# Three kinds of PSUM evictions, written as ScalarE's

## The chip, the cores and the metric

One core of a Trainium2 chip runs the whole program. Five engines share it, each with an in-order instruction queue of its own: TensorE (PE in the profile, with its weight loads as PEld), VectorE (DVE), ScalarE (ACT), GpSimd (POOL) and SyncE (SP, which here only issues DMAs). The metric is the device time of one execution in microseconds; the median over several runs counts.

## What is computed

Two sequences of 1024 positions with 256 features pass through four residual blocks, each behind a layer norm: causal attention with 16 heads of width 128 and ALiBi slopes, a gated FFN with ternary weights, a Mamba block (a state space with 512 channels and 16 states), and a gated FFN that keeps the two largest of every four hidden values.

```python
def reference(...):
    x = L0_attn_resid_pre                                   # (2, 1024, 256), fp32
    x = x + _L0_attn_ref(_layernorm(x), Wq, Wk, Wv, Wo)
    x = x + _L0_ffn_ref(_layernorm(x), w_gate_up, w_proj)
    x = x + _L1_attn_ref(_layernorm(x), in_proj, conv1d, x_proj, dt_proj, ...)
    x = x + _L1_ffn_ref(_layernorm(x), w_gate, w_up, w_down)
    return x

# attention, the block that the change touches
q, k, v = (resid_pre @ W.T).reshape(b, s, H, DH)            # for Wq, Wk, Wv
scores = clip(einsum('bqhd,bkhd->bhqk', q, k) / sqrt(DH), -1024, 1024)
attn = softmax(scores + alibi_mask)
z = einsum('bhqk,bkhd->bqhd', attn, v)
out = einsum('bqhd,ohd->bqo', z, Wo.reshape(d, H, DH))
```

## The kernel before

The 2048 positions are cut into four chunks `k` of 512 (two for each sequence; the second one of a sequence has `u = 1` and attends to twice as many keys). Attention runs over 64 heads, chunk by chunk (`attention`). The other three blocks of a chunk (`rest`: `ternary_ffn`, `state_space`, `kept_two_ffn`) are interleaved with the attention of the next chunk: the main loop gives attention one query tile of 128 positions and then lets `rest` go on until its share of a hand-written cost is spent. While chunk 0 is in attention, the ternary weights are quantized instead. The `rest` of the last chunk has no attention beside it and forms the tail.

For one query tile `j` of a head, `scores` makes the products on TensorE (L362), clips them on VectorE into `ss` (L366), adds the bias and takes the row maximum on VectorE (L372, `nm`) and the exponential on ScalarE (L377). Two tiles later `turn` transposes these weights on TensorE, block by block (L293, into a PSUM bank `pt`), and copies each bank to SBUF, `pT` (L296): one copy of up to four 128-blocks, or two copies where a row has more than four. After the fourth tile `values` multiplies `v` and `pT` (L304, bank `z`) and copies the bank to `zs` (L309). `project` multiplies `zs` with `wo` (L318) and adds to the residual on VectorE (L324). `qkv` makes `q`, `k` and `v` of the next head (L335, L342); `q` and `k` leave their banks by a ScalarE activation (L338), `v` by a copy (L347).

The banks of `pt`, `z`, `o`, `pq`, `pk` and `pv` are one ring of three (`ps_mm`), those of `s` a ring of two, and the banks of the other blocks a ring of two (`ps_r`). In a gated FFN (`glu`) the gate and the up product take one bank each of `ps_r`: the next gate product waits until ScalarE has read this one (L446, Silu into `sg`), the next up product until VectorE has multiplied (L447). In `ternary_ffn` ScalarE then also makes the high half `hh` (L479) and the squares `sq` (L483, L486), and the products take both halves `hh` and `hl`. In `state_space` each of 64 steps takes an exponential on ScalarE (`da`, L750), a scan on VectorE (`hs`, L757) and two products on GpSimd (`db` L736, `hc` L771).

ScalarE's functions live in table sets. Silu (L446, L629, L632) is in another set than the exponential (L377, L750), and where they alternate in ScalarE's queue the compiler puts a table load in front (ACT_TABLE_LOAD). No load stands in front of a plain copy in this trace.

The order within each queue is not written out by hand. The tracer of the tile framework schedules the recorded instructions on an estimate of its own, and an instruction that was written for "any" engine is given to ScalarE or to VectorE by this schedule. Beside the three lines of the change, the turned layer norm (L148), `dtls` (L643) and `bc` (L656) are copies for "any" engine too.

Of the kernel before, what the change touches and what calls it, by code (L numbers as in the profile page):

```python
# [17 lines left out]
P = 128  # L18
# [23 lines left out]
def kernel(  # L42
# [21 lines left out]
    nc = tc.nc  # L64
# [221 lines left out]
    def turn(k, h, j, s, st):  # L286

        qi = CH[k][1] * UT + j
        for kb0 in range(0, qi + 1, 4):
            n = min(4, qi + 1 - kb0)  # L290
            tp = ps_mm(f"pt_{k}_{h}_{j}_{kb0}").rearrange("p (c t) -> p c t", c=4)
            for i in range(n):
                nc.tensor.transpose(  # L293
                    tp[:, i, :], s[:, (kb0 + i) * P : (kb0 + i + 1) * P], ident
                )
            nc.any.tensor_copy(st["pts"][kb0 // 4][:, 0:n, j * P : (j + 1) * P], tp[:, 0:n, :])  # L296

    def values(k, h, st):
        u = CH[k][1]
        zp = ps_z(f"z_{k}_{h}")  # L300
        last = (u + 1) * UT - 1
        for kb in range(last + 1):
            q0 = max(0, kb - u * UT) * P
            nc.tensor.matmul(  # L304
                zp[:, q0:], lhsT=st["v_all"][:, kb, :],
                rhs=st["pts"][kb // 4][:, kb % 4, q0:], start=(kb == 0), stop=(kb == last),
            )
        st["z"] = a2.tile([P, U], F32, tag="z", name=f"zs_{k}_{h}")
        nc.any.tensor_copy(st["z"], zp)  # L309

    def project(k, h, st):

# [15 lines left out]
    def qkv(k, h, st, xT):  # L328
        u = CH[k][1]
        st["qT"] = a2.tile([P, U], F32, tag="qT", name=f"qT_{k}_{h}")  # L330
        kT = st["kT"][:, u * U : (u + 1) * U]
        for n, dst, scale in (("q", st["qT"], -1.0 / math.sqrt(DH)), ("k", kT, 1.0)):
            pp = ps_mm(f"p{n}_{k}_{h}")
            for c in range(KC):
                nc.tensor.matmul(  # L335
                    pp, lhsT=st[n][:, c, :], rhs=xT[:, c, :], start=(c == 0), stop=(c == KC - 1)
                )
            nc.scalar.activation(dst, pp, AF.Copy, scale=scale)  # L338
        vp = ps_mm(f"pv_{k}_{h}").rearrange("p (t m) -> p t m", t=UT)
        for t in range(UT):  # L340
            for c in range(KC):
                nc.tensor.matmul(  # L342
                    vp[:, t, :], lhsT=xT[:, c, t * P : (t + 1) * P], rhs=st["v"][:, c, :],
                    start=(c == 0), stop=(c == KC - 1),
                )
        v = st["v_all"][:, u * UT : (u + 1) * UT, :]
        nc.any.tensor_copy(v, vp)  # L347
        if u < NU - 1:
            kd = dr.tile([P, U], F32, tag="kd", name=f"kd_{k}_{h}", bufs=H)
            nc.sync.dma_start(out=kd, in_=kT)  # L350
            vd = dr.tile([P, UT, DH], F32, tag="vd", name=f"vd_{k}_{h}", bufs=H)
            nc.sync.dma_start(out=vd, in_=v)
            kept[CH[k][0], h] = kd, vd
# [28 lines left out]
    def attention():  # L382
# [3 lines left out]
        for k in range(1, len(CH)):  # L386
            load_x(k)
        qkv(0, 0, live[0], xns[0])
        later = []
        for i, (k, h) in enumerate(heads):  # L390
# [8 lines left out]
            for j in range(UT):  # L399
                s = scores(k, h, j, st)  # L400
                later.append((LAG, lambda a=(k, h, j, s, st): turn(*a)))
                if j == UT - 1:
                    later.append((LAG, lambda a=(k, h, st): values(*a)))
                    later.append((LAG + 1, lambda a=(k, h, st): project(*a)))
                if j == UT - 1 and h == H - 1:
                    for _, f in later:
                        f()
                    later = []
                else:
                    now = [f for n, f in later if n == 0]  # L410
                    later = [(n - 1, f) for n, f in later if n]
                    for f in now:
                        f()
                if j == 1 and i + 1 < len(heads):
                    qkv(*heads[i + 1], live[0], xns[heads[i + 1][0]])
                if j == 0 and h == H - 1 and k + 1 < len(CH):

                    with tc.issue_after(tiles[-UT].ins) if k == 0 else nullcontext():
                        normed(k + 1)
                yield k  # L420
# [627 lines left out]
```

## Time and profile before

| what | value |
| --- | --- |
| median of 3 runs (range) | 1835.89 us (1833.85 to 1839.79) |
| span of the profiled execution | 1836.9 us |
| ACT busy, DVE busy, POOL busy | 963.7 (52%), 1218.3 (66%), 832.2 us (45%) |
| L309 `zs` copies, ACT and DVE | 52 and 12 |
| L347 `v` copies, ACT and DVE | 58 and 6 |
| DVE time of the copies, L296, L309, L347 | 35.31, 8.27, 4.13 us |
| table loads before L377, before L446 | 28 and 26, 1283 ns each |
| HBM traffic | 138 GB/s over the span |

The busy share of an engine is a mean over stages with different limits, so the profile is read in stages. The stages follow from the lines: the ternary FFN of chunk 0 has its gate and up products from 243.8 to 278.6 us, that of chunk 2 from 1135.5 to 1164.9 us; the scans of the state space run from about 363.7 to 588.2 us (chunk 0), 832.6 to 1013.5 us (chunk 1) and 1252.4 to 1476.2 us (chunk 2); the tail begins at about 1613 us. A matmul's record is longer than the time after which the next one can start, so TensorE's true need is counted from start to start.

### The profile page before, as it was taken

The numbers are of one execution on the slowest core, as the hardware profiler recorded it, in microseconds if no ns is written. First come the engines' busy times: TensorE is split into PE (matmuls) and PEld (weight loads), VectorE is DVE, ScalarE is ACT, GpSimd is POOL, SyncE is SP. The second block draws the span as 40 slices with busy tenths as digits, with TensorE's granted clock in tenths as the row PEclk, the third lists the DMA queues.
The fourth block names the chain that finished last, engine by engine and source line by source line (L and its number), as shares of the span: only waits on it lengthen the run. The fifth ranks groups of instructions, "written<-read, shape, count | busy, mean of one in ns | idle before, by whom it ended". The sixth has DMA issues, their size and how long they took to land. (4 is left out here: it accounts for less than half of the span.)

```text
span 1836.9 us, 24217 instructions
## 1 busy us (share of the span) xinstructions
PE 1718.3 (94%) x7956; PEld 1144.2 (62%) x7956; DVE 1218.3 (66%) x2349; ACT 963.7 (52%) x1789; POOL 832.2 (45%) x674
## 2 busy tenths in 40 slices
PE   7999999998999999998888999999999999998899
PEld 4666666555656557755555667756656565566895
DVE  5666555777785473458886565557788655667975
ACT  3444474656563553555554545566555446446742
POOL 3324032588892000419998000418898500035870
PEclk9999999999999999999999999999999999999999
DMA  6443512466662311337787324227665430212541
GB/s 201 128 142 128 193 46 88 149 203 204 216 202 91 103 52 48 125 109 232 245 247 224 116 71 141 82 67 228 226 214 184 142 115 26 75 53 86 178 136 57
DMA packets 178301, 255.99 MB, mean 139 GB/s; under 512 B 16240, under 2 KB 90992, under 8 KB 177152
## 3 DMA queue, kind: packets, MB, share of 16 engines
q1 hardware_dynamic: 176752, 241.61, 41.4%
q0 software_dynamic: 1152, 12.58, 1.9%
q8 instruction: 63, 1.03, 0.2%
q14 instruction: 62, 0.51, 0.1%
q10 hardware_dynamic: 272, 0.26, 0.0%
HBM read 232.04 MB, written 22.35 MB: 138 GB/s over the span
## 5 line engine op out<-in xcount | busy, mean ns | idle before, releaser
L771 POOL TENSOR_TENSOR hc<-hs,cs 128x512 f32<-128x512 f32 x256 | 362.1, 1428 | 10.8 <-DVE ss L366 3.1
L362 PE MATMUL s<-kT,qT 128*128 128x512 f32 (+3 forms) x768 | 302.7, 495 | 19.9 <-DVE ss L366 18.0
L377 ACT ACTIVATE ss<-ss,nm 128x128 f32<-128x128 f32 (+7 forms) x256 | 198.8, 776 | 183.5 <-DVE nm L372 174.1
L366 DVE SCALAR_TENSOR_TENSOR ss<-s,lower 128x512 f32<-128x512 f32 (+3 forms) x384 | 204.6, 549 | 121.0 <-PE s L362 119.4
L736 POOL TENSOR_TENSOR db<-du,bs 128x512 f32<-128x512 f32 x192 | 259.2, 1356 | 44.4 <-DVE hs L757 30.6
L304 PE MATMUL z<-pT,v 128*128 128x512 f32 (+3 forms) x768 | 264.5, 492 | 10.9 <-ACT pT L296 10.2
L372 DVE CUSTOM_DVE_ANT_0 ss<-ss,alibi 128x128 f32<-128x128 f32 (+7 forms) x256 | 241.3, 945 | 3.5
L750 ACT ACTIVATE da<-dl,a_neg 128x512 f32<-128x512 f32 x256 | 177.9, 698 | 115.6 <-DVE hs L757 90.6
L304 PEld LDWEIGHTS z<-pT,v 128*128 128x128 f32 x768 | 142.8, 190 | 145.1 <-issue 92.7
L296 ACT COPY pT<-pt 128x512 f32<-128x512 f32 (+3 forms) x321 | 145.4, 474 | 162.0 <-PE pt L293 160.4
L293 PE MATMUL pt<-ident,ss 128*128 128x128 f32 x1152 | 180.3, 279 | 32.1 <-DVE x L324 18.5
L293 PEld LDWEIGHTS pt<-ident,ss 128*128 128x128 f32 x1152 | 140.0, 142 | 94.7 <-DVE x L324 33.0
L362 PEld LDWEIGHTS s<-kT,qT 128*128 128x128 f32 x768 | 127.9, 193 | 84.1 <-issue 43.4
L757 DVE TENSOR_TENSOR_SCAN hs<-da,db 128x512 f32<-128x512 f32 x128 | 153.8, 1210 | 38.6 <-ACT da L750 20.8
L757 DVE TENSOR_TENSOR_SCAN hs<-da,carry,db 128x512 f32<-128x512 f32 x128 | 159.1, 1269 | 24.4 <-POOL hc L771 14.7
L324 DVE SCALAR_TENSOR_TENSOR x<-o,rr,x 128x256 f32<-128x256 f32 x256 | 108.9, 476 | 76.7 <-PE o L318 76.5
L701 PE MATMUL y<-ident,hc 128*128 128x128 f32 x1024 | 144.8, 279 | 8.4 <-POOL hc L771 8.4
L342 PEld LDWEIGHTS pv<-wv,xT_a 128*128 128x128 f32 x1024 | 124.4, 192 | 37.1 <-issue 25.3
L342 PE MATMUL pv<-wv,xT_a 128*128 128x128 f32 x1024 | 125.8, 275 | 5.5 <-ACT zs L309 3.4
L701 PEld LDWEIGHTS y<-ident,hc 128*128 128x128 f32 x1024 | 121.0, 145 | 14.3 <-POOL hc L771 11.9
L318 PE MATMUL o<-wo,zs 128*128 128x256 f32 x512 | 125.4, 386 | 4.1 <-ACT kT L338 3.0
L335 PE MATMUL pq<-xT_a,wq 128*128 128x512 f32 x256 | 122.7, 601 | 0.7 <-ACT xT_a L148 0.7
(204 smaller groups left out, 2468.7 us busy)
## 6 DMA issues: line engine op xcount, KB each, us to landing
cs<-bcd SPq DMA_DIRECT2D x256, 256.0 KB, 3.8
bs<-bcd SPq DMA_DIRECT2D x192, 256.0 KB, 4.3
alibi<-alibi_d SPq DMA_DIRECT2D x32, 512.0 KB, 4.2
wq<-in_wqT_dram SPq DMA_DIRECT2D x64, 128.0 KB, 3.5
wk<-in_wkT_dram SPq DMA_DIRECT2D x64, 128.0 KB, 3.1
wv<-in_wvT_dram SPq DMA_DIRECT2D x64, 128.0 KB, 2.8
wo<-in_woT_dram SPq DMA_DIRECT2D x64, 128.0 KB, 2.8
alibi<-alibi_d SPq DMA_DIRECT2D x32, 256.0 KB, 3.6
```

The lines of the kernel that those rows point to most:

```text
L293: nc.tensor.transpose(tp[:, i, :], s[:, (kb0 + i) * P : (kb0 + i + 1) * P], ident)
L304: nc.tensor.matmul(zp[:, q0:], lhsT=st["v_all"][:, kb, :], rhs=st["pts"][kb // 4][:, kb % 4, q0:], start=(kb == 0), stop=(kb == last),)
L342: nc.tensor.matmul(vp[:, t, :], lhsT=xT[:, c, t * P : (t + 1) * P], rhs=st["v"][:, c, :], start=(c == 0), stop=(c == KC - 1),)
L362: nc.tensor.matmul(sp[:, :n], lhsT=st["qT"][:, j * P : (j + 1) * P], rhs=st["kT"][:, k0 : k0 + n], start=True, stop=True,)
L366: nc.vector.scalar_tensor_tensor(s[:, k0 : k0 + n], sp[:, :n], CLIP, lower[:, S - W + k0 : S - W + k0 + n], op0=ALU.min, op1=ALU.max,)
L372: pace["tile"] = nc.vector.tensor_tensor_reduce(out=s[:, :W], in0=s[:, :W], in1=st["alibi"][:, :W], scale=1.0, scalar=3.0e38, op0=ALU.add, ...
L377: nc.scalar.activation(s[:, :W], s[:, :W], AF.Exp, bias=nm, scale=-1.0, accum_out=st["rs"][:, j : j + 1])
L701: nc.tensor.matmul(yTs[c][:, t * P : (t + 1) * P], lhsT=h[:, t * P : (t + 1) * P], rhs=ident, is_transpose=True, start=start and t == 0, s ...
L736: nc.gpsimd.tensor_tensor(db[i], du, brow.pop(i), ALU.mult)
L750: nc.scalar.activation(da[i], parts[c][0], AF.Exp, scale=a_neg[:, c, n : n + 1])
L757: nc.vector.tensor_tensor_scan(out=hs[i], data0=da.pop(i), data1=db.pop(i), initial=0.0 if first else carry[:, n, c : c + 1], op0=ALU.mult ...
L771: nc.gpsimd.tensor_tensor(hc[i], hs.pop(i), crow.pop(i), ALU.mult)
```

## The change

The copies of L296, L309 and L347 are written for ScalarE. Nothing else is changed in the source.

```diff
@@ turn
-            nc.any.tensor_copy(st["pts"][kb0 // 4][:, 0:n, j * P : (j + 1) * P], tp[:, 0:n, :])
+            nc.scalar.copy(st["pts"][kb0 // 4][:, 0:n, j * P : (j + 1) * P], tp[:, 0:n, :])
@@ values
-        nc.any.tensor_copy(st["z"], zp)
+        nc.scalar.copy(st["z"], zp)
@@ qkv
-        nc.any.tensor_copy(v, vp)
+        nc.scalar.copy(v, vp)
```

Since the tracer schedules all queues anew, the two built programs differ in more than these copies. Counted over the queues of the two programs (program order, no times):

| instructions | before | after |
| --- | --- | --- |
| L296 on ACT / on DVE | 321 / 63 | 384 / 0 |
| L309 on ACT / on DVE | 52 / 12 | 64 / 0 |
| L347 on ACT / on DVE | 58 / 6 | 64 / 0 |
| L148, L643, L656 on DVE | 1, 0, 0 | 2, 2, 2 |
| table loads before L377 / before L446 | 28 / 26 | 37 / 33 |
| table loads in all | 66 | 82 |
| matmuls on PE | the same | the same, in another order in places |

GpSimd's and SyncE's queues have the same instructions as before.

## The prediction

> **What bounds the kernel now.** First the page's line of busy times, then the busy times by stage, then the chains of records inside two stages.
>
> ```profile
> PE 1718.3 (94%) x7956; PEld 1144.2 (62%) x7956; DVE 1218.3 (66%) x2349; ACT 963.7 (52%) x1789; POOL 832.2 (45%) x674
> ```
>
> TensorE is the resource in short supply. Counted from start to start its need is 0.86 us for a 128x512 fp32 product (two `pq` products start at 236.69, `pk` follows at 238.41), 0.23 for a ternary one (245.20 to 245.43), 0.11 for a transpose (eight from 256.21 to 257.08). Over the program's own list of matmuls that is some 1640 us; the span has 197 us more. The stages say where these are.
>
> ```profile
> 243.80:278.60 34.80, 34.80 (x149) 23.48 (x148) 17.47 (x32) 31.11 (x45) 16.94 (x13) 1.00 0.15 46
> ...
> 363.70:588.20 224.50, 206.19 (x1002) 136.35 (x1000) 170.21 (x303) 124.54 (x228) 176.25 (x126) 1.00 0.60 189
> ...
> 1135.50:1164.90 29.40, 29.40 (x122) 20.38 (x123) 12.62 (x23) 23.73 (x37) 15.61 (x13) 1.00 0.14 41
> ```
>
> Columns: stretch, its length, busy time of PE, PEld, DVE, ACT, POOL, granted clock, DMA share, GB/s. In the ternary FFN of chunks 0 and 2 PE is never idle: by the prices above its list there needs 34.1 and 29.0 us against 34.8 and 29.4 measured. But ACT is busy for 31.1 of 34.8 us: nearly a second bound. In the state space of chunk 0 nobody is full (PE's list needs 199 of 224.5 us, POOL 176, DVE 170, ACT 125); chunk 2 looks the same, and in chunk 1 (832.6 to 1013.5) POOL with 166.6 of 180.9 us is the bound. These three stages lose 25, 50 and 25 us of PE.
>
> Why ACT is so busy in the FFN:
>
> ```profile
> 244.61 1.28 ACT L446 ACT_TABLE_LOAD   x1
> 245.91 0.60 ACT L446 ACTIVATE sg_f<-g_f 128x512 f32<-128x512 f32 x1
> 246.71 1.28 ACT L377 ACT_TABLE_LOAD   x1 [0.20 <-DVE nm L372]
> 248.00 1.05 ACT L377 ACTIVATE ss<-ss,nm 128x896 f32<-128x896 f32 x1
> 248.95 0.19 ACT L377 ACTIVATION_READ_ACCUMULATOR ss<-ss,nm 128x1 f32 x1
> 249.04 0.60 ACT L479 CAST hh<-h 128x512 fp32r<-128x512 f32 x1
> 249.55 0.63 ACT L483 ACTIVATE ss<-h 128x512 f32<-128x512 f32 x1
> 250.20 1.28 ACT L446 ACT_TABLE_LOAD   x1
> ```
>
> Each Silu that stands between two exponentials costs two table loads of 1.28 us.
>
> **The change, part by part.** 81 copies leave DVE, where they took 47.7 us (35.31 + 8.27 + 4.13). On ACT a 128x512 copy takes 0.585 us against 0.66 to 0.69, so ACT gets some 42 us and stands at 55%.
>
> ```profile
> L296 ACT COPY pT<-pt x321: 242/486/601, 25.6 to 1597.2; 128x512 f32<-128x512 f32 x84, 128x128 f32<-128x128 f32 x28, 128x256 f32<-128x256 f32 x25, 128x384 f32<-128x384 f32 x24
> L296 DVE COPY pT<-pt x63: 276/660/693, 42.3 to 1597.7; 128x512 f32<-128x512 f32 x33, 128x256 f32<-128x256 f32 x14, 128x384 f32<-128x384 f32 x10, 128x128 f32<-128x128 f32 x6
> ```
>
> *FFN of chunk 0.* Here DVE had six `pT` and one `zs` copy; all go to ACT, and the new order of ACT's queue has an exponential between nearly all Silus: 12 table loads from the first Silu to the last, before 8. From the first Silu up to the sixth (`sg_5`) the new queue holds 10 loads (12.83 us), 6 Silus (3.51), 5 exponentials of 640 to 1024 with the read of their sum (5.46), 5 pairs of `hh` and `sq` (5.30, start to start) and 8 `pT` (4.04): 31.1 us, and the first Silu begins 0.9 us after the stage, when its gate product is made. The ring of two banks lets the seventh gate product start only after `sg_5`, at 32.0. PE's order has 11.1 us behind it (two steps of eight ternary products 3.7, the end of `z` 2.2, `pq` and `pk` 3.4, `pv` 1.7). So the stage takes at least 43.1 us where PE needs 36.5: 6.6 us of stall. The same sum on the old queue gives 32.3, under PE's 34.1, and the stage was indeed PE's. After the stage PE lost 4.6 us before (21.8 us to the first `in` product of L608, 17.2 by the list), part of it behind exponentials that now come earlier; I give back 1.5. **+5**, bounds +2 (more given back) and +9 (waits of ACT on DVE and PE, taken as none).
>
> *FFN of chunk 2.* 10 loads instead of 4. Up to `sg_5`: 12.83 + 3.51 + 5.57 + 5.30 + 1.65 + 0.9 = 29.8, and 8.0 of PE behind: 37.8 against 32.1. 5.7, less 1.5: **+4**, bounds +1 and +8.
>
> *Gated FFN of chunks 0 and 2.* Two loads more each, 5.1 us. ACT then needs 38.1 and 33.4 us where PE needs 52.3 and 51.7, and at no Silu does ACT's sum plus PE's remainder exceed PE's own. **0**, covered by the fp32 products; +5.1 uncovered. Chunk 1 has the same loads as before, the last chunk no attention.
>
> *The copy of `v` in the state spaces.*
>
> ```profile
> DVE v L347 <- PE pv L342: 24.6, 4, 8.0
> ```
>
> Four times (438, 495, 1326, 1383 us) DVE stood in front of this copy; in the first case:
>
> ```profile
> 429.84 0.27 DVE L766 COPY carry<-hs 128x1 f32<-128x1 f32 x2
> 438.06 0.69 DVE L347 COPY v<-pv 128x512 f32<-128x512 f32 x1 [7.96 <-PE pv L342]
> 438.67 1.22 DVE L757 TENSOR_TENSOR_SCAN hs<-da,db 128x512 f32<-128x512 f32 x1
> ```
> ```profile
> 436.28 0.60 ACT L338 ACTIVATE kT<-pk 128x512 f32<-128x512 f32 x1 [1.12 <-PE pk L335]
> 436.77 0.69 ACT L750 ACTIVATE da<-dl,a_neg 128x512 f32<-128x512 f32 x1
> ```
>
> Queued behind the copy are the scans, on which `hc` and `da` wait. That looks like 8 us to be won, but the scan also needs its `da`, which sits in ACT's queue behind `kT`, done at 437.46. In the new queue `v` stands on ACT ahead of this `da`: 438.06 + 0.59 + 0.69 = 439.3 for the scan instead of 438.67. The wait only changes engine: 4 x 0.65 = **+2.6**, bounds -4.8 (4 x 1.2, were `da` issued first) and +6.
>
> *The other DVE copies in the state spaces:* 16 `pT` and 2 `zs`, 2.33 + 3.13 + 2.25 + 0.68 + 0.68 = 9.1 us off a DVE at 76 to 80%; ACT at 55% takes them ahead of some `da`. A third of it: **-3**, bounds -9.1 and +4. POOL, the bound of chunk 1, gets nothing from it.
>
> *Elsewhere* (attention beside the quantizing, gated FFNs, 45 copies, 0.1 us shorter each) PE has work queued: **0**, bounds -4 and +3. The five copies of L148, L643, L656 that go to DVE lie in stretches where it idles: 0.
>
> *The clock.*
>
> ```profile
> 1165.00:1175.00 10.00, 8.84 (x40) 7.21 (x40) 4.69 (x11) 3.73 (x6) 4.93 (x4) 0.73 0.01 3
> ```
>
> Waits of under 1 us each, 1.16 in all, were here followed by a clock of 0.73: some 2.7 us of the 10 were lost. The new stalls in two FFNs are larger. **+1**, bounds 0 and +5.4 (one such stretch in each).
>
> Sum: 5 + 4 + 2.6 - 3 + 1 = +9.6 on 1836.9 us of span. The median of the runs lies 1.0 below this span, and I take the same offset: 1845.5, rounded 1846.
>
> [...]
>
> **The rivals.** (a) *The loads stay hidden.* For it: ACT idles over 40% of the span, and PE's queue differs in each stage. It needs the 12.3 us of computed stalls to be absorbed after the stages, where PE lost 4.6 and 7.3 us. Then 2.6 - 3 remain: 1836. (b) *DVE's relief wins, faster.* In the state spaces of chunks 0 and 2 PE had three waits after each blocked `v` (1.62, 1.25 and 0.92 us after 438, the same after the other three): 15.2 us. If these go because DVE can scan during the 8 us, and the 9.1 us of copies count in full, it is -24.3 + 9 from the FFNs: 1821. For it: `pt` and `s` wait for DVE (L324 and L366) there. Against: `da` on ACT. It decides once more than about 15 us come back. (c) *Every new load on the path.* 16 x 1.28 = 20.5, with the clock's 5.4: 1862. For it: the queues are in order, and each stalled Silu delays `hh`, `hl` and the exponentials. Against: PE's longer fp32 stages. That the change doesn't do what it says is excluded by the programs: no copy of these lines is left on DVE.
>
> **How the numbers follow.** Forecast 0.49 (1841 to 1852), (a) 0.21, (b) 0.16, (c) 0.14. The range 1832 to 1861 leaves out most of (b) and the end of (c). A difference under 0.3% (5.5 us, as the three runs spread over 0.32%) can't be told from none. Slower: 0.49 and 0.14, less 0.01, 0.62; same 0.22; faster 0.16.
>
> **What would show it.** The stage from the first to the last product of the FFN of chunk 0 takes 43 to 46 us, that of chunk 2 38 to 41, with ACT over 90% busy and PE waiting for `sg_f`; the gated FFNs keep their 51 us; the scans at the four places come 0.6 us later and ACT waits for `pv`. Wrong if these FFN stages stay under 38 and 33 us, or if the state spaces of chunks 0 and 2 move by more than 5 us each.

## The result, and the profile after

The changed kernel takes 1866.05 us (median of 4 runs, 1864.28 to 1873.3), the kernel before 1834.87 us (4 runs, 1833.11 to 1839.79). The ratio is 1.0172, with an interval of [1.0148, 1.0196]: slower by some 31 us, where 1846 was forecast and the range ended at 1861. The profiled executions have spans of 1836.9 and 1865.0 us, 28.1 apart; the stages below are cut from these two.

The busy times of the page after:

```profile
PE 1725.6 (93%) x7956; PEld 1146.0 (61%) x7956; DVE 1192.2 (64%) x2273; ACT 1007.0 (54%) x1881; POOL 827.1 (44%) x674
```

ACT has 43 us more and DVE 26 us less. That the forecast gave ACT 42 us is partly luck, as it counted the copies alone. The durations of ACT's records add up to 58 us more, 20.5 of them the 16 new table loads; the busy time counts records that overlap once. Neither says where 28 us went: ACT still idles for 46% of the span. So the span is cut at TensorE's landmarks (first and last product of each block), and the pieces are set side by side:

| piece (chunk) | before | after | difference | forecast |
| --- | --- | --- | --- | --- |
| ternary FFN (0) and up to the first `in` | 34.8 + 21.8 | 44.9 + 18.7 | +6.9 | +5 |
| ternary FFN (2) and up to the first `in` | 29.4 + 24.5 | 41.1 + 20.4 | +7.5 | +4 |
| opening of the state space, first `in` to the scans (0, 2) | 63.2, 63.0 | 65.3, 65.9 | +2.1, +2.8 | none |
| scans (0, 1, 2) | 224.5, 180.9, 223.8 | 225.7, 182.6, 226.1 | +1.2, +1.7, +2.3 | -0.4 in all |
| gated FFN (0, 2) and up to the next ternary FFN | 51.2 + 79.0, 50.6 + 55.7 | 52.7 + 78.1, 52.0 + 53.9 | +0.6, -0.3 | 0 |
| from the gated FFN (1) to the ternary FFN (2) | 58.3 | 60.6 | +2.3 | 0 |
| everything else | | | +1.0 | 0 |

The forecast's +1 for the clock lies within the two FFN rows here. Half of the loss is where it was expected, and half is not.

A longer stage isn't always a loss. The two gated FFNs are 1.5 us longer each, but TensorE has no gap in them, before or after (chunk 0; the columns are those of the prediction's stages: stretch, length, busy time of PE, PEld, DVE, ACT, POOL, granted clock, DMA share, GB/s):

```profile
617.70:668.90 51.20, 51.20 (x172) 27.63 (x173) 27.13 (x56) 33.92 (x46) 1.01 (x1) 1.00 0.22 69
628.70:681.40 52.70, 52.70 (x177) 28.38 (x178) 27.11 (x56) 37.56 (x52) 1.01 (x1) 1.00 0.21 67
```

The new order has five more products in the stage, attention's `s` among them, and the stretch behind it is shorter by 0.9 and 1.8 us. So the two are taken together in the table, and little is lost there.

The stages of the two ternary FFNs and of the scans of chunk 0, after the change:

```profile
244.50:289.40 44.90, 40.22 (x155) 25.54 (x155) 20.36 (x33) 41.51 (x60) 18.13 (x13) 0.96 0.17 53
1151.60:1192.70 41.10, 36.28 (x135) 24.06 (x135) 15.15 (x29) 36.05 (x51) 18.05 (x13) 0.88 0.15 49
373.40:599.20 225.80, 206.09 (x1002) 136.78 (x1001) 170.22 (x295) 125.58 (x235) 173.79 (x126) 1.00 0.59 187
```

Before, PE was never idle in the two FFN stages (busy for 34.8 of 34.8 and 29.4 of 29.4 us). Now it has no work for 4.7 and 4.8 us, and ACT is busy for 92% and 88%: in these two stages the bound has gone over to ACT. What was waited for in the first of them (engine and tile, releaser: us in total, times, longest):

```profile
POOL hl L481 <- ACT hh L479: 27.2, 7, 8.9
DVE h L447 <- ACT sg_f L446: 8.7, 3, 5.7
PEld g_f L441 <- ACT sg_f L446: 5.2, 4, 3.8
...
PE g_f L441 <- ACT sg_f L446: 3.6, 1, 3.6
```

All four wait for ACT, and three of them for a Silu. Its queue shows why (start, us, engine, line, operation, tile):

```profile
273.09 1.28 ACT L377 ACT_TABLE_LOAD   x1
274.38 1.04 ACT L377 ACTIVATE ss<-ss,nm 128x896 f32<-128x896 f32 x1
275.33 0.18 ACT L377 ACTIVATION_READ_ACCUMULATOR ss<-ss,nm 128x1 f32 x1
275.54 1.28 ACT L446 ACT_TABLE_LOAD   x1
276.83 0.60 ACT L446 ACTIVATE sg_f<-g_f 128x512 f32<-128x512 f32 x1
277.44 1.28 ACT L377 ACT_TABLE_LOAD   x1
278.74 1.15 ACT L377 ACTIVATE ss<-ss,nm 128x1024 f32<-128x1024 f32 x1
```

In these 6.8 us ACT makes two exponentials and one Silu, and spends 3.8 us on loads. The table loads over the whole span (count, busy us, mean ns, idle time before them):

```profile
L377 ACT ACT_TABLE_LOAD x37 | 47.5, 1283 | 1.5 <-DVE nm L372 0.9
L446 ACT ACT_TABLE_LOAD x33 | 42.3, 1283 | 1.1 <-PE g_g L441 0.6
```

They were 28 and 26. Ten of the 16 new ones stand in the two ternary FFNs, four in the gated FFNs of chunks 0 and 2, and one in each opening of their state spaces. The copies of `pT` are now all ACT's:

```profile
L296 ACT COPY pT<-pt x384: 241/536/608, 26.0 to 1626.0; 128x512 f32<-128x512 f32 x128, 128x128 f32<-128x128 f32 x32, 128x384 f32<-128x384 f32 x32
```

The place in the scans where DVE had stood in front of `v`, in DVE's queue and then in ACT's:

```profile
440.89 0.27 DVE L766 COPY carry<-hs 128x1 f32<-128x1 f32 x2
449.17 1.22 DVE L757 TENSOR_TENSOR_SCAN hs<-da,db 128x512 f32<-128x512 f32 x1 [8.01 <-ACT da L750]
```
```profile
446.10 0.60 ACT L338 ACTIVATE kT<-pk 128x512 f32<-128x512 f32 x1 [1.12 <-PE pk L335]
447.89 0.58 ACT L347 COPY v<-pv 128x512 f32<-128x512 f32 x1 [1.19 <-PE pv L342]
448.37 0.70 ACT L750 ACTIVATE da<-dl,a_neg 128x512 f32<-128x512 f32 x1
```

The wait of 8 us is still there. DVE stands in front of the scan now, because the scan's `da` is queued on ACT behind `v`, and `v` waits for TensorE.

The opening of the state space, for which the prediction has no term, before and then after:

```profile
334.64 0.60 ACT L632 ACTIVATE sz<-in 128x512 f32<-128x512 f32 x1
335.26 1.28 ACT L636 ACT_TABLE_LOAD   x1
```
```profile
341.97 1.08 ACT L632 ACTIVATE sz<-in 128x512 f32<-128x512 f32 x2
343.07 1.28 ACT L377 ACT_TABLE_LOAD   x1
344.37 0.83 ACT L377 ACTIVATE ss<-ss,nm 128x640 f32<-128x640 f32 x1
345.10 0.19 ACT L377 ACTIVATION_READ_ACCUMULATOR ss<-ss,nm 128x1 f32 x1
345.19 0.94 ACT L296 COPY pT<-pt 128x512 f32<-128x512 f32 x2
346.16 1.28 ACT L636 ACT_TABLE_LOAD   x1
```

Before, the load for L636 stood right behind the last Silu. Now an exponential of attention with a load of its own and two `pT` copies stand between, and that load comes 3.1 us after the last Silu (346.16 less 343.05). The product `dtl` starts 34.5 us after the first `in` product instead of 33.1, and the first `da` comes at 46.2 instead of 44.5.

At the end of the gated FFN of chunk 1 no load is new, but a copy stands behind one now. Before, VectorE made it; after, ACT does, and TensorE waits (before, then ACT's and TensorE's queue after):

```profile
1078.05 0.69 DVE L296 COPY pT<-pt 128x512 f32<-128x512 f32 x1
```
```profile
1091.82 1.28 ACT L377 ACT_TABLE_LOAD   x1
...
1094.70 0.57 ACT L296 COPY pT<-pt 128x512 f32<-128x512 f32 x1
```
```profile
1095.32 2.42 PE L304 MATMUL z<-pT,v 128*128 128x512 f32 x8 [1.95 <-ACT pT L296]
```

The transposes that this copy waits for start at 1077.41 us before and at 1091.27 after: the copy follows them by 0.6 us on VectorE and by 3.4 on ACT. This wait is most of the 2.3 us of that row.

### The profile page after: what moved, and what is told of

Same layout as the page of the kernel before. It is cut to its first block, busy times and chain, and to the rows that moved or that the text cites. A ratio compares the mean times of both kernels' runs of the same rounds, so it can differ in the third digit from the quotient of the medians.

```text
span 1865.0 us, 24205 instructions
## 1 busy us (share of the span) xinstructions
PE 1725.6 (93%) x7956; PEld 1146.0 (61%) x7956; DVE 1192.2 (64%) x2273; ACT 1007.0 (54%) x1881; POOL 827.1 (44%) x674
## 4 chain that ended last, share of the span: by engine, by line
PE 57%; DVE 16%; ACT 8%; POOL 8%; issue 6%; DMA 5%; SPq 0%; POOLq 0%; DVEq 0%; ACTq 0%
PE z L304 11%; PE s L362 6%; PE pv L342 5%; PE pq L335 4%; DVE hs L757 4%; PE pk L335 4%; DVE ss L372 4%; POOL hc L771 3%; PE in L608 3%; PE o L318 3%; PE pt L293 3%; DMA bs<-bcd 3%; PE g_g L441 3%; PE u_g L441 3%; POOL db L736 3%
## 5 line engine op out<-in xcount | busy, mean ns | idle before, releaser
L771 POOL TENSOR_TENSOR hc<-hs,cs 128x512 f32<-128x512 f32 x256 | 349.2, 1376 | 12.5 <-PE y L701 4.0
L362 PE MATMUL s<-kT,qT 128*128 128x512 f32 (+3 forms) x768 | 298.4, 495 | 10.9 <-DVE ss L366 10.6
L377 ACT ACTIVATE ss<-ss,nm 128x128 f32<-128x128 f32 (+7 forms) x256 | 198.3, 775 | 190.7 <-DVE nm L372 175.2
L736 POOL TENSOR_TENSOR db<-du,bs 128x512 f32<-128x512 f32 x192 | 266.1, 1393 | 52.3 <-DMA bs<-bcd 19.7
L304 PE MATMUL z<-pT,v 128*128 128x512 f32 (+3 forms) x768 | 269.7, 501 | 16.4 <-ACT pT L296 15.7
L372 DVE CUSTOM_DVE_ANT_0 ss<-ss,alibi 128x128 f32<-128x128 f32 (+7 forms) x256 | 254.7, 997 | 5.4
L296 ACT COPY pT<-pt 128x512 f32<-128x512 f32 (+3 forms) x384 | 171.3, 476 | 158.6 <-PE pt L293 156.9
L757 DVE TENSOR_TENSOR_SCAN hs<-da,carry,db 128x512 f32<-128x512 f32 x128 | 159.3, 1270 | 27.9 <-POOL hc L771 18.7
```

The source lines that it names most:

```text
L304: nc.tensor.matmul(zp[:, q0:], lhsT=st["v_all"][:, kb, :], rhs=st["pts"][kb // 4][:, kb % 4, q0:], start=(kb == 0), stop=(kb == last),)
L362: nc.tensor.matmul(sp[:, :n], lhsT=st["qT"][:, j * P : (j + 1) * P], rhs=st["kT"][:, k0 : k0 + n], start=True, stop=True,)
L372: pace["tile"] = nc.vector.tensor_tensor_reduce(out=s[:, :W], in0=s[:, :W], in1=st["alibi"][:, :W], scale=1.0, scalar=3.0e38, op0=ALU.add, ...
L377: nc.scalar.activation(s[:, :W], s[:, :W], AF.Exp, bias=nm, scale=-1.0, accum_out=st["rs"][:, j : j + 1])
L736: nc.gpsimd.tensor_tensor(db[i], du, brow.pop(i), ALU.mult)
L757: nc.vector.tensor_tensor_scan(out=hs[i], data0=da.pop(i), data1=db.pop(i), initial=0.0 if first else carry[:, n, c : c + 1], op0=ALU.mult ...
```

## The experiments

Each was timed beside the kernel before on the same chip, in three rounds; that kernel's medians there were 1837.1 to 1838.3 us, so a ratio says more than a time. The letters of the theories are those of the expectations. A is the view of the prediction, enlarged: table loads between Silus cost time wherever ACT sets the pace, and the place of `v` does the rest.

### Where: the three copies by stage

A helper chooses the engine by the block of `rest` that runs beside the attention.

```diff
+    phase = {"at": None}                  # "f", "m", "g" while ternary_ffn, state_space, kept_two_ffn run
+    def evict(dst, src):
+        (nc.any.tensor_copy if phase["at"] in ('f',) else nc.scalar.copy)(dst, src)
...
-            nc.any.tensor_copy(st["pts"][kb0 // 4][:, 0:n, j * P : (j + 1) * P], tp[:, 0:n, :])
+            evict(st["pts"][kb0 // 4][:, 0:n, j * P : (j + 1) * P], tp[:, 0:n, :])
```

(and so for L309 and L347). The first is as shown: "any" beside the ternary FFN, ScalarE elsewhere.

> The three copies are ScalarE's as in the changed kernel, but left to any engine while a ternary FFN runs beside the attention. Theory A (ScalarE's queue in the two ternary FFN stages, where table loads for nearly every Silu make it the bound): these two stages go back to 35 and 29.5 us, with the stretch behind them 14.4 us are regained of the changed kernel's 1866: 1852 (1847 to 1856). Theory B (every copy moved to ScalarE costs about the same wherever it stands): only 10 of the 81 copies return, 4 us: 1862.

Measured: 1852.43 us, ratio 1.0075 [1.0055, 1.0095]. The FFN stages are back at 34.8 and 29.4 us; the gated FFNs keep 52.7 and 52.0, the openings 64.8 and 65.1, the scans 225.8 and 225.8. So the ternary FFNs hold about half of the loss, and the rest is in the other blocks.

The second is the opposite: ScalarE beside the ternary FFN, "any" elsewhere.

> The three copies are ScalarE's only while a ternary FFN runs, and left to any engine elsewhere. Theory A: the two stages take 44.9 and 41.1 us as in the changed kernel, the rest is as before: 1835 + 14.4 = 1849 (1845 to 1854). Theory B: 10 copies of 81 moved, 1835 + 4 = 1839.

Measured: 1854.37 us, ratio 1.0095 [1.0068, 1.0122]. The FFN stages are 44.9 and 40.3 us, openings and gated FFNs within 0.2 us of those before. The median is 5 us over A's figure; by the ratio, A's 14.4 us lie inside the interval (12.5 to 22.4). The profile doesn't explain the median: it is of the longest of the four executions (1861.68 us), and what that one has beyond the median is in one place, the scans of chunk 2 with 231.0 us, 6.8 of them at half clock from 1435 us. Such a piece came in one more profile, that of the kernel before without tables (e9 below), in the scans of chunk 0 (a clock of 0.66 from 530 to 540 us); that was the longest execution of its kernel too.

The third has "any" in the state space and ScalarE elsewhere (`phase["at"] in ('m',)`).

> The three copies are ScalarE's but left to any engine while a state space runs. Theory A: the two ternary FFN stages stay at 45 and 41 us, the two gated ones at 52.5 and 52; the openings and the scans of the state spaces go back to the times of the kernel before (63, 224.5, 63, 224), 10 us of the 31: 1855 (1852 to 1859).

Measured: 1857.15 us, ratio 1.0097 [1.0075, 1.012]. Openings 63.5 and 63.0, scans 224.5 and 223.8: both as before. The FFNs keep their stall, 45.7 and 41.0, the gated ones the changed kernel's order, 52.7 and 52.2.

### Why: table loads, or the copies themselves

If ACT stalls the FFN because of its copies, the stall stays when the loads go. So Silu, before which 26 loads stand in `glu` (33 in the changed kernel), is replaced there by a plain copy, first in the kernel before and then in the changed one:

```diff
-            nc.scalar.activation(sg, g_ps, AF.Silu)
+            nc.scalar.activation(sg, g_ps, AF.Copy)
```

> The kernel before with a Copy in the place of Silu in both gated FFNs (it leaves this function out), so that ScalarE never changes its table there: 17 table loads in all instead of 66. Both theories: the FFN stages were PE's before, so little is won: 1826 to 1836. It is the base of the next run.

> The changed kernel with a Copy in the place of Silu in both gated FFNs (it leaves this function out): 19 table loads instead of 82. Theory A, with the table loads as the cause inside the two ternary FFN stages: these stages are within 1.5 us of those of the base run, and the time is 10 to 16 us over it (the part of the 31 us that lies outside these stages and outside the gated FFNs). Theory C (the copies' own time ahead of the Silus, not the loads, makes these stages longer): they stay 4 to 7 us each over the base run, and the time 25 us or more.

Measured: 1836.52 us, ratio 0.9997 [0.9987, 1.0008] for the kernel before; 1848.69 us, ratio 1.006 [1.0043, 1.0077] for the changed one. The difference of the two is 12.2 us instead of 31.2. Of the changed kernel, the two FFN stages:

```profile
243.60:278.80 35.20, 34.37 (x148) 23.30 (x148) 14.68 (x24) 22.15 (x43) 17.48 (x13) 1.00 0.14 44
1142.30:1172.50 30.20, 30.20 (x129) 20.95 (x129) 10.79 (x21) 18.97 (x36) 16.25 (x13) 1.00 0.14 40
```

They are 1.1 and 1.6 us longer than in its partner without Silu (34.1 and 28.6), with all the copies still on ACT; ACT's busy time fell from 41.5 to 22.2 us and from 36.1 to 19.0. So the copies alone don't stall the FFNs. The edit takes more than the loads away, though: the schedule comes out anew, and 631 of TensorE's 7956 products stand at another place than in the changed kernel. In the gated FFNs, back at 51.2 and 50.6, it is just this: the five products are in their old place. The stretch ahead of the ternary FFN of chunk 2 is back at 58.5 us too. For the ternary FFNs ACT's own records speak for the loads. From the first to the end of the sixth Silu ACT took 30.8 us in the changed kernel, with 0.5 us of idle time and 12.8 us of loads; without these its sum would be 18, where TensorE needs 25 up to there (36.5 less 11.1, by the prediction's list). In the kernel before, on the other hand, 49 loads fewer (66 to 17) win nothing in the whole, and 0.7 and 0.8 us in the two FFN stages: there TensorE's queue covered nearly all of them.

The remaining loads, of the Silus of L629 and L632 in the state space, go too (the same edit there); each program then has 5 loads in all.

> The kernel before with a Copy in the place of every Silu, those of the state space too (it leaves this function out): 5 table loads in the whole program. 1833 to 1839, and the base of the next run.

> The changed kernel with a Copy in the place of every Silu (it leaves this function out): 5 table loads. Theory A: the opening of the state spaces of chunks 0 and 2, which in the changed kernel takes 2.1 and 2.8 us longer with one table load more, is within 0.5 us of the base run, and of the 31 us 4 to 8 are left (the order of v and da in the state spaces, and small shifts). Theory F (the copies in ScalarE's queue delay what stands behind them, loads or not): the opening stays 2 us longer and 10 to 14 us are left.

Measured: 1837.87 us, ratio 0.9993 [0.9977, 1.0008], and 1841.65 us, ratio 1.0016 [0.9998, 1.0034]. The difference is 3.8 us, and the openings are 63.6 and 63.6 us against 63.1 and 63.0. So the differences go 31.2, 12.2, 3.8, each to some 4 us by the intervals of the ratios: some 19 us go with the loads beside `glu`, some 8 with the loads beside the state space, and some 4 are not loads. Of the 8 the profiles show 3, in the two openings (2.1 and 2.0 us over the partner with these loads, 0.5 and 0.7 without); where the rest was isn't shown.

### How many loads, or which

A count of loads would be an easy rule. VectorE takes the copies beside the ternary FFN, which still gives 80 loads (`nc.vector.tensor_copy` in `'f'`, "any" elsewhere).

> The three copies are VectorE's while a ternary FFN runs and left to any engine elsewhere. The tracer then puts even more table loads into ScalarE's queue in all, 80 instead of 66 (the changed kernel has 82), but with the copies gone ScalarE's sum up to the sixth Silu plus TensorE's remainder is 32.8 and 30.3 us where TensorE itself needs 34.8 and 30.8. Theory A (a load costs only where ScalarE's sum passes TensorE's): the two stages take 35.5 and 31.5 us, the whole 1835 to 1841. Theory D (each added load costs its 1.28 us, or most of it): 14 loads, 1850 to 1855.

Measured: 1847.17 us, ratio 1.0049 [1.0033, 1.0065]. The FFN stages:

```profile
244.30:280.20 35.90, 35.80 (x152) 24.34 (x151) 22.12 (x39) 32.49 (x45) 15.70 (x12) 1.00 0.14 45
1145.50:1177.50 32.00, 32.00 (x140) 22.45 (x138) 16.38 (x32) 28.12 (x42) 16.87 (x13) 1.00 0.12 37
```

PE has almost no gap, and the stages are 1.0 and 2.6 us longer than before (A 35.5 and 31.5); the stretches behind them are shorter by as much, 20.6 and 22.1 us instead of 21.8 and 24.5. They have two and four of the 14 new loads. Seven more are in the ternary FFN of chunk 1:

```profile
747.50:778.10 30.60, 30.60 (x133) 21.96 (x132) 15.44 (x36) 25.93 (x42) 14.21 (x11) 1.00 0.19 65
```

This stage took 21.6 us before, but here too PE has no gap: 36 more products, of attention, lie in it. So 13 loads more held up TensorE in none of these stages, which refutes a price for each load. The whole lies between A's figure and D's all the same, 6 us over A's: chunk 1, from its ternary FFN to the end of its scans, took 272.1 us instead of 265.5. Its scans took 189.2 instead of 180.9, with GpSimd busy for 174.5 us instead of 166.6 and a granted clock of 0.90 instead of 0.94. Whether the new order ahead of them did that wasn't tried.

### Which of the three lines

One line each for ScalarE, the other two for "any".

> Only the copy of the turned weights (L296) is ScalarE's, z and v are left to any engine. The queue of ScalarE has the 82 table loads of the changed kernel. Theory A: the two FFN stages are those of the changed kernel, 44 to 45 and 40 to 41 us, and the time is 1858 to 1866.

Measured: 1865.6 us, ratio 1.0148 [1.013, 1.0166], with 82 loads, FFN stages of 44.9 and 40.3 us, openings of 65.0 and 65.1, scans of 225.8 and 225.9, gated FFNs of 52.7 and 52.0. The copy of `pT` alone brings nearly all of it.

> Only the copy of z (L309) is ScalarE's. Table loads stay at 66. Theory A: no stage changes its bound, 1833 to 1841. Theory B (each copy moved costs its share of the 31 us): 12 of 81 copies, 1839 to 1842.

Measured: 1839.11 us, ratio 1.0009 [0.9998, 1.0021]. No stage changes.

> Only the copy of v (L347) is ScalarE's. Table loads stay at 66. Theory A: in the state spaces of chunks 0 and 2 the wait of 8 us before this copy changes its engine, and the scan behind it comes 0.65 us later at four places: these two stages 0.5 to 2 us longer each, the whole 1836 to 1841. Theory E (VectorE freed of four waits of 8 us): up to 15 us faster, 1822 to 1832.

Measured: 1833.73 us (10 runs, 1830.73 to 1837.79), ratio 0.9978 [0.9967, 0.9989]. This one beats both kernels, against what was expected of it: the scans of chunks 0 and 2 took 222.0 us each, instead of 224.5 and 223.8. Its ACT queue and its DVE queue at the first of the four places:

```profile
435.62 0.60 ACT L338 ACTIVATE kT<-pk 128x512 f32<-128x512 f32 x1 [1.12 <-PE pk L335]
436.11 0.69 ACT L750 ACTIVATE da<-dl,a_neg 128x512 f32<-128x512 f32 x1
437.40 0.59 ACT L347 COPY v<-pv 128x512 f32<-128x512 f32 x1 [0.60 <-PE pv L342]
```
```profile
429.19 0.27 DVE L766 COPY carry<-hs 128x1 f32<-128x1 f32 x2
436.90 1.22 DVE L757 TENSOR_TENSOR_SCAN hs<-da,db 128x512 f32<-128x512 f32 x1 [7.44 <-ACT da L750]
```

Here the schedule put `da` ahead of `v`. The scan starts 1.28 us after `kT` does; before it was 2.39 (438.67 less 436.28), in the full change 3.07 (449.17 less 446.10). Four places at 1.11 us make 4.4 us, and the two stages together are 4.3 us shorter.

Is it this order? The same kernel, with `da` held behind `v` at these four places:

```diff
-        nc.any.tensor_copy(v, vp)
+        pace["v"] = nc.scalar.copy(v, vp)
...
-                nc.scalar.activation(da[i], parts[c][0], AF.Exp, scale=a_neg[:, c, n : n + 1])
+                with tc.issue_after(pace["v"].ins) if paced and n == 9 and c in (1, 2) else nullcontext():
+                    nc.scalar.activation(da[i], parts[c][0], AF.Exp, scale=a_neg[:, c, n : n + 1])
```

> The kernel with only v's copy on ScalarE, with one order forced: at heads 7 and 9 of chunks 1 and 3 the exponential da that the next scan needs comes behind the copy of v instead of ahead of it. TensorE's queue is the same instruction for instruction, all others are the same but for this. Theory A: the scan behind comes 1.75 us later at four places; the state spaces of chunks 0 and 2 take 224.5 to 226 us instead of 222.0, the whole 6 to 8 us more than with da ahead. Theory G (other shifts of the order made the kernel with only v faster): they stay at 222.

Measured: 1839.36 us, ratio 1.001 [0.9994, 1.0026]. The scans take 225.1 and 224.6 us, and ACT's queue has the order of the full change:

```profile
436.94 0.60 ACT L338 ACTIVATE kT<-pk 128x512 f32<-128x512 f32 x1 [1.12 <-PE pk L335]
438.72 0.58 ACT L347 COPY v<-pv 128x512 f32<-128x512 f32 x1 [1.19 <-PE pv L342]
439.20 0.70 ACT L751 ACTIVATE da<-dl,a_neg 128x512 f32<-128x512 f32 x1
```

By the medians the order at these four places is worth 5.6 us, by the two stages 5.7 (2.6 in chunk 2; 3.1 in chunk 0, with 3.4 us at half clock). The copy's engine was the same in both, and so is TensorE's whole queue. Not all else is the same, as had been expected: at these places the schedule also put the next `da` and `pT` the other way round and moved a scan and some of attention's steps in VectorE's queue. So what e7 gains is shown to be the order at these places, with `da` ahead of `v` as its start; the two neighbours alone weren't separated from what followed them.

## Why the prediction was right and wrong

*The ternary FFNs.* The mechanism and the stage times were right: 44.9 us (43 to 46 said) and 41.1 (38 to 41 said), with ACT at 92% and 88% (over 90 said) and PE waiting for `sg_f`. The terms were still too small, +6.9 and +7.5 instead of +5 and +4, 5.4 short together, or 4.4 with the clock's +1. The sum of ACT's queue from the first to the end of the sixth Silu was right: 30.8 and 28.8 us, where 31.1 and 28.9 were said. Mis-sized is what stands ahead of it and behind it. The first Silu begins 2.2 and 3.1 us after the stage does, instead of 0.9, because a copy and a table load are ahead of it in ACT's queue; in chunk 2, with the stage from 1151.6:

```profile
1152.78 0.59 ACT L296 COPY pT<-pt 128x512 f32<-128x512 f32 x1 [1.24 <-PE pt L293]
1153.39 1.28 ACT L446 ACT_TABLE_LOAD   x1
1154.68 0.60 ACT L446 ACTIVATE sg_f<-g_f 128x512 f32<-128x512 f32 x1
```

Behind the sixth Silu the stages took 12.0 and 9.2 us, where 11.1 and 8.0 of PE were summed. What was given back behind the stages was about right: of the 3.1 and 4.1 us there, 2.4 and 3.1 are work of PE that the new order has already done in the stage (36.5 less 34.1 and 32.1 less 29.0).

*The clock.* This stretch is in the second FFN stage:

```profile
1167.00:1177.20 10.20, 7.58 (x16) 4.78 (x16) 0.69 (x1) 10.11 (x15) 5.10 (x5) 0.50 0.14 49
```

At this clock of 0.50 the ternary products start 0.43 us apart (1167.55 to 1167.98), instead of 0.23 just ahead of it (1166.35 to 1166.58). By the granted clock of the two stages, 44.9 x 0.04 = 1.8 and 41.1 x 0.12 = 4.9 us of PE's pace are lost, where the kernel before had 1.00 in both. Little of that reached the time, because ACT set the pace: it was busy for 10.11 of the 10.2 us. The second stage took 40.3 us in e2 and in e6, at granted clocks of 0.96 and 0.92, and 41.0 in e12 at 0.88; ACT needed 28.8 us up to the sixth Silu in all of them. So some 0.8 us of the 4.9 counted. Behind this stage both kernels have a lower clock: 0.86 over 24.5 us before, 3.4 us lost, and 0.92 over 20.4 us after, 1.6 lost. Around the two FFNs that is 0.8 more inside and at most 1.8 less behind, in place of +1.

*The steps that failed.* The forecast was +9.6, and the spans differ by 28.1. Of the 18.5 us between them, 4.4 are the FFN terms above, and three steps of the prediction have 12.8. The first is the term of "*The other DVE copies in the state spaces*", **-3**: with the one of `v` it gave -0.4 for the scans, which took 5.2 us more, so 5.6 are missing. The second is that the openings of state spaces 0 and 2 had no term at all: they took 2.1 and 2.8 us more, and without tables only 0.5 and 0.7 (e10 against e9). The table counts on record (before L377, 28 to 37; before L446, 26 to 33) were spread over the FFNs alone, and the one load more in each opening was not asked for. The third is "*Elsewhere*", where "PE has work queued" gave **0**: it has the 2.3 us ahead of the ternary FFN of chunk 2, where a `pT` copy that had been DVE's stands behind a load. The last 1.3 us are spread over other pieces. The term for the gated FFNs, **0**, held: PE has no gap there, and their 1.5 us more are mainly products that came from behind them.

*The other DVE copies, -3.* Nothing of it came. Of the 3.5 us in chunks 0 and 2, e11 has 0.6 and 0.8, with `v` ahead of `da` as in the full change and the other copies as before. So the step of `v` cost some 1.4 us and not 2.6, and the other 2.1 us came with the `pT` and `zs` copies that were to win 3. Work that left a DVE at 76 to 80% gave PE nothing: DVE's long waits there are for ACT (`da`, 25.8 us in chunk 0), which got the copies. The 1.7 us of chunk 1 are not in e1 and e6 (180.9 and 181.1 us), which have the same copies on ACT there, so they are probably of this execution.

*The copy of `v`* was read rightly: the wait changed its engine, and the scan starts 0.68 us later after `kT` (3.07 against 2.39; 0.65 forecast). The lower bound, 4 x 1.2 us gained "were `da` issued first", is what e7 showed: 4.3 us. For e7 itself the opposite order was expected, which the queue of the built program would have answered.

*The rivals.* (a) fell with the FFN stages, and (b), the faster side, with the scans, which gave nothing back. (c), every new load on the path, came nearest with 1862, but not by its reason: ten new loads in the ternary FFNs went with 14.4 us, two in the openings with 4.9, four in the gated FFNs with 0.3, and in e5 13 held up PE in none of the FFN stages. In these runs, what a load cost went with whether ACT's sum up to the next function that others wait for goes past PE's. As the range was drawn up to (c)'s figure, which has no price for the exponentials and copies that come with a load, it ended 5 us under the result.

## What to carry to other kernels

Where a tracer schedules, a copy's new engine can re-order other queues; read the built queues, and count table loads and what stands between them for each stage, also for those that the change doesn't touch. In these runs a load of 1.28 us cost next to nothing as long as another engine had work queued (49 fewer gave a ratio of 0.9997), and about its own time or more where a ring of banks waited for the function behind it (14.4 us with ten of them). Before a longer stage is called a loss, count the products in it and look for gaps: the gated FFNs were 1.5 us longer and lost next to nothing. The same goes for a low clock: in the FFN of chunk 2, where ACT set the pace, some 0.8 of the 4.9 us of PE's pace reached the time. Look for the one line that does good: pinning `v` alone gives 0.9978 [0.9967, 0.9989], pinning `pT` alone 1.0148 [1.013, 1.0166], and with the first it is the order at four places that counts, `da` ahead of `v` in ACT's queue.

## What was not expected of the hardware

49 table loads fewer, 63 us of ACT's time, changed nothing in the time of the kernel before (0.9997 [0.9987, 1.0008]): here ACT's busy time didn't tell what they cost.

The clock stood at 0.50 for 10.2 us in the FFN of chunk 2 (1167.0 to 1177.2), where the prediction's row has 0.73 over 10 us, and PE had records for 74% of this time (7.58 us). One wait of PE, of 2.19 us, ended at 1166.02, ahead of this stretch; the next, of 2.62 us, ended at 1171.66, within it. What makes the clock fall, and for how long, no run here shows.
